# Layer 1's u for the later batches: block products of two levels instead of one, with its steps moved between the products of layer 2

## The chip, the core and the metric

The kernel runs on one core of a Trainium2 chip. The metric is the device time of one execution in microseconds (us). The kernel before took 1878.11 us, the median of three runs (1877.98 to 1878.81). The profiled execution took 1878.7 us; the span between its first and its last instruction is 1876.8 us, and the clock granted to TensorE was 0.999 of full speed.

## The reference

The input x has shape (8, 512, 32, 32): eight batches, 512 channels, 1024 positions, all in float32. Four layers follow each other. Layer 0 mixes the channels through a small attention whose matrix is divided by its largest singular value. Layer 1 is group norm and attention over the 1024 positions, layer 2 a projection to 3 x 128 channels with an attention of its own, layer 3 a convolution with signs as weights. The part that matters here is layer 1:

```
h = _group_norm(x, gamma, beta).reshape(B, C, N)
q = jnp.einsum('oc,bcn->bon', wq, h) + bq[None, :, None]
k = jnp.einsum('oc,bcn->bon', wk, h) + bk[None, :, None]
logits = jnp.einsum('bcn,bcm->bnm', q, k) * scale
attn = jax.nn.softmax(logits, axis=-1)
```

The kernel doesn't form q and k one by one. It multiplies the two weights once into a 512 x 512 matrix wu and computes, for each batch, u = wu h + bias, a 512 x 1024 matrix; the logits are then the product of u and h.

## The kernel before, in words

Up to about 184 us the kernel loads the input, computes layer 0's statistics and the combined weights. Then `fast` (line 911) runs once for each of the eight batches, and for each it runs these stages in turn: layer 1's scores (`scores1`), its value projection (`make_v`), its value products (`values1`, line 566), layer 2's projection (`project2`, line 658), layer 2's scores (`scores2`, line 826), its value products (`values2`, line 981), and layer 3 with the output (`leave`, line 705), half of which is put off into the next batch.

u of batch n+1 is made while layer 2 and layer 3 of batch n run. `make_u` (line 490) is a generator: each `next` issues one step. In `fast` it stands as `steps`, and `fill()` (line 966) asks it for a step at places that the code names: after the last projections of `project2`, after every second row block of `scores2`, before `values2`, between the parts of `leave`, and what is left at the end of the batch. In batch 0 u of the first batch is made ahead of the loop.

Large products are not computed directly. A product of two matrices is cut into 2 x 2 blocks and done with seven block products instead of eight: `sums_of` (line 318) makes the sums of the left factor's blocks (S1 to S4), `differences_of` those of the right factor's (T1 to T4), and `seven` (line 342) issues the seven products and joins them. The seven terms are A11 B11, A12 B21, S1 T1, S2 T2, S3 T3, S4 B22 and A22 T4. Some are summed in place in PSUM: the bank `pa` first takes A11 B11, ScalarE copies it out (`move`), then S2 T2 is added into the same bank and it is copied out again, and so on. `move` runs on ScalarE (lines 350 and 352), `plus`, which adds a bank to what lies in SBUF, on VectorE (lines 356 and 358). For u, `make_u` works on two groups of 128 rows; each of its 14 steps is one term with a contraction of 256, that is two matmuls of 128 x 128 by 128 x 512, and the matmul instructions all have line 405 (`product_of`).

All eight PSUM banks stand in one pool with the tag `bank`. A scheduler orders the instructions of each engine: it follows the program's order as long as operands are ready, and issues what comes later in the program when something before it would have to wait. The order in which it leaves them is then fixed; on the chip each engine works its list off in that order and waits where an operand isn't there. Semaphores guard a PSUM bank as a whole: a product into one half of a bank waits for a reading of the other half.

wu and the sums su of its blocks lie in the pool of the weights for the whole kernel. A fallback at the end (`general`), which runs only if a check on the softmax sums fails, uses wu too.

Of the kernel before, what the change touches and what calls it, by code (L numbers as in the profile page):

```python
# [16 lines left out]
P = 128  # L17
B = 8
C = 512
# [66 lines left out]
def kernel(  # L86
# [157 lines left out]


    r_dram = [dram.tile([4, N // 4], F32, name=f"r_dram{i}") for i in range(2 * B)]
    f_dram = [dram.tile([P, HF], F32, name=f"f_dram{b}") for b in range(B)]
    gm = [keep.tile([P, P], F32, tag=f"gm{j}", name=f"gm{j}") for j in range(NPAIR)]
    gs_, gh_ = (
# [18 lines left out]

    wu = wpool.tile([P, CC, C], F32, tag="wu", name="wu")
# [5 lines left out]
    su = wpool.tile([P, 3, 2, C // 2], F32, tag="su", name="su")  # L277
    so = wpool.tile([P, 3, 2, C // 2], F32, tag="so", name="so")


# [209 lines left out]
    def make_u(env, hb, got, early=False):  # L490
# [32 lines left out]
        for g in groups:  # L523
            yield from g

    def make_v(hb, vt):
# [131 lines left out]
    def project2(env, xt, made):  # L658


        big = env["big"]
        tpg = big.tile([P, 3, N], F32, tag="us", name="tpg")
        tt, pt = tpg[:, 0:1, :], tpg[:, 1:2, :]
        gt = tpg[:, 2, :].rearrange("p (t c) -> p t c", c=P)
        wa = weights["tp"]
        xb = differences_of(
            [xt[:, chunks[k], half(n)] for k in range(2) for n in range(2)],
            [env["e"].tile([P, 2, HF], F32, tag="e", name="xd") for i in range(4)],
        )
        term = product_of(lambda a, b, q, k: wa[a][:, k, :], lambda a, b, q, k: xb[b][:, k, :])  # L670
        yield from seven(
            term,
            tt[:, 0, half(0)],
            tt[:, 0, half(1)],
            pt[:, 0, half(0)],
            pt[:, 0, half(1)],
            col("L2_conv_W_b", 0),
            col("L2_conv_W_b", 1),
        )
        for h in reversed(range(NH)):  # L680
            ps = bank().rearrange("p (t c) -> p t c", c=P)
            for i in range(4):
                for cc in range(CC):
                    mm(  # L684
                        out=ps[:, i, :],
                        lhsT=xt[:, cc, bass.ts(4 * h + i, P)],
                        rhs=sbw["tpg"][:, cc, 2 * P : 3 * P],
                        start=cc == 0,
                        stop=cc == CC - 1,
                    )  # L690
            nc.vector.tensor_tensor(
                gt[:, bass.ts(h, 4), :], ps, bg_row.unsqueeze(1).to_broadcast([P, 4, P]), ALU.add
            )
            yield
        made.extend((tt, pt, gt))
# [130 lines left out]
    def scores2(env, pt, tt, fill):  # L826
        es, esum = [], None
        for t in range(NT):
            e = env["e"].tile([P, N], F32, tag="e", name="e")
            for h in range(NH):  # L830
                ps = bank()
                mm(  # L832
                    out=ps,
                    lhsT=pt[:, 0, bass.ts(t, P)],
                    rhs=tt[:, 0, half(h)],
                    start=True,
                    stop=True,
                )
# [72 lines left out]
    def fast(env, n, hb, ua):  # L911
# [12 lines left out]
        for k, _ in enumerate(scores1(env, hb, ua, es)):  # L924
            if rest3 and k % 2 == 0:
                if next(rest3[0], "end") == "end":
                    rest3.pop()
                    if more and order[n + 1] not in resident:
                        resident[order[n + 1]] = load_x(order[n + 1])
            if n == 0 and k == 2:  # L930
                weights["o"] = sums_of(quarters_of(wo, chunks, cols2), [so[:, i] for i in range(3)], True)
            if n == 0 and k == 6:
# [22 lines left out]
        for k, _ in enumerate(values1(env, xt, vt, es, r, scratch)):  # L955
            chore(k in (2, 7, 9, 11, 13))
            if k == 5 and more:
                nxt = resident[order[n + 1]]
                hb = split_h(env, normal(env, nxt))
        signs = None  # L960
        if more:
            steps = make_u(env, hb, got)
        else:
            signs = unpacked(env)

# [611 lines left out]
    def filler():  # L1577

        yield from natural("v", "k")
        load_w("p", w_p, [P, CC, C], a1, tag="v")
        yield from product(nat["q"], nat["k"], wu, True)
        for b in order[:2]:
# [12 lines left out]
        yield from product(nat["v"], sbw["p"], wo, False)  # L1597
# [35 lines left out]
    with ExitStack() as main:  # L1633
# [8 lines left out]
        for _ in make_u(env, hb, got, True):  # L1642
            pass
        ua = got[0]
        for n in range(B):
            hb, ua = fast(env, n, hb, ua)

# [113 lines left out]
    with tc.If(verdict[0] > 0):  # L1761
        with (
# [5 lines left out]
            env = {"big": big, "e": epool, "small": small}  # L1768
            psum_pools(stack, 2, 4)

            for a in (weights["u"], weights["o"]):
                nc.vector.tensor_tensor(a["S3"], a["A11"], a["S3"], ALU.subtract)
            for b in range(B):
                xt = load_x(b)
                general(env, xt, b, channels(out[b]))
# [42 lines left out]
```

## Time and profile before

| what | value | where it is read |
|---|---|---|
| time, median of three runs | 1878.11 us | the runs |
| time of the profiled execution | 1878.7 us | the profile |
| span of the profiled execution | 1876.8 us | head of the page |
| TensorE busy with matmuls (PE) | 1856.3 us, 99% | part 1 of the page |
| VectorE busy (DVE) | 1118.4 us, 60% | part 1 |
| ScalarE busy (ACT) | 545.4 us, 29% | part 1 |
| GpSimd busy (POOL) | 121.9 us, 6% | part 1 |
| line 405, right factor h, left factor wu (u) | 192 matmuls, 88.9 us busy | groups |
| moved by DMA | 66.51 MB, mean 35 GB/s | part 2 |

A row of the timeline gives the start, the duration, the engine, the line, the operation, the tile that is written and those that are read, the shape and how often it follows itself; in brackets, how long the engine had been idle and what ended that. PE is the matmul, PEld the load of the stationary operand, which runs beside the matmul before. A matmul of the code is two instructions in the trace, so a step of `make_u` is a row with x4. "us, mean ns" of a group are the time in which one or more of its instructions ran, and the mean duration of one; matmuls overlap, so the time from one start to the next is shorter than the duration.

### The profile page before, as it was taken

To read this page: it belongs to the slowest core of one execution; us is meant where nothing else is said; L and a number is where in the kernel's file an instruction comes from. 1 tells how busy PE (TensorE), PEld (TensorE's weight loads), DVE (VectorE), ACT (ScalarE), POOL (GpSimd) and SP (SyncE) were. 2 spreads that over 40 slices of the span, in tenths; PEclk is the share of its full clock that TensorE was granted. 3 is DMA by queue.
4 is the path that set the end of the run, shared out by engine and by line. 5 is a ranking of instruction groups with operands and counts; after the bars stand their busy time and mean duration, and the time that the engine had idled before them with its cause. 6 is when DMAs were issued, how large, how long until landed. Compare 5 with 4: busy or idle time off the path is not lost.

```text
span 1876.8 us, 16564 instructions
## 1 busy us (share of the span) xinstructions
PE 1856.3 (99%) x6244; PEld 952.5 (51%) x6244; DVE 1118.4 (60%) x2077; ACT 545.4 (29%) x888; POOL 121.9 (6%) x109
## 2 busy tenths in 40 slices
PE   9999999999999999999999999999999999999997
PEld 3456465544645455544645455544645464544653
DVE  3347687467754777567764676457643666355447
ACT  2142221244202521244202522144202521244113
POOL 1000001100020001100020001100020001000011
PEclk9999999999999999999999999999999999999999
DMA  8420000002000200002000200001000200000001
GB/s 323 164 79 7 1 18 1 1 34 73 12 1 12 90 18 1 0 34 73 12 1 12 88 19 0 1 34 67 12 0 12 90 12 0 1 34 23 12 0 47
DMA packets 25202, 66.51 MB, mean 35 GB/s; under 512 B 3552, under 2 KB 4764, under 8 KB 24476
## 3 DMA queue, kind: packets, MB, share of 16 engines
q1 hardware_dynamic: 24188, 64.96, 9.6%
q8 instruction: 51, 0.84, 0.2%
q10 hardware_dynamic: 864, 0.43, 0.1%
q14 instruction: 35, 0.29, 0.0%
q0 software_dynamic: 64, 0.00, 0.0%
HBM read 46.44 MB, written 18.94 MB: 35 GB/s over the span
## 4 chain that ended last, share of the span: by engine, by line
PE 96%; DVE 2%; ACT 1%; DMA 0%; issue 0%; POOL 0%; DVEq 0%; ACTq 0%
PE bank L405 46%; PE bank L583 21%; PE bank L832 6%; PE bank L985 5%; PE bank L1372 4%; PE bank L684 3%; PE bank L701 3%; PE bank L429 2%; PE bank L724 1%; PE wide L1417 1%; PE bank L1053 1%; PE bank L1473 1%; PE bank L855 0%; PE quad L1266 0%; PE bank L1563 0%; PE bank L1159 0%
## 5 line engine op out<-in xcount | busy, mean ns | idle before, releaser
L583 PE MATMUL bank<-e,vt 128*128 128x512 f32 x768 | 336.2, 594 | 0.0
L583 PEld LDWEIGHTS bank<-e,vt 128*128 128x128 f32 x768 | 144.3, 190 | 172.3 <-issue 167.9
L405 PE MATMUL bank<-ut,h 128*128 128x512 f32 x384 | 178.9, 597 | 0.0
L405 PEld LDWEIGHTS bank<-ut,h 128*128 128x128 f32 x384 | 71.3, 190 | 94.7 <-issue 93.0
L405 PE MATMUL bank<-us,hs 128*128 128x512 f32 x256 | 115.6, 593 | 0.0
L832 PE MATMUL bank<-tpg 128*128 128x512 f32 x256 | 115.4, 595 | 0.0
L985 PE MATMUL bank<-e,tpg 128*128 128x512 f32 x256 | 114.7, 595 | 0.0
L356 DVE TENSOR_TENSOR e<-bank,e 128x512 f32<-128x512 f32 x96 | 66.1, 689 | 60.8 <-PE bank L405 45.1
L839 ACT ACTIVATE e<-bank 128x512 f32<-128x512 f32 x128 | 76.3, 597 | 67.0 <-PE bank L832 67.0
L350 ACT COPY e<-bank 128x512 f32<-128x512 f32 x96 | 56.2, 585 | 118.8 <-PE bank L405 118.5
L405 PE MATMUL bank<-wo,h 128*128 128x256 f32 x384 | 89.9, 384 | 0.0
L405 PE MATMUL bank<-h,wu 128*128 128x512 f32 x192 | 88.9, 594 | 0.0
L985 PEld LDWEIGHTS bank<-e,tpg 128*128 128x128 f32 x256 | 48.1, 190 | 60.4 <-issue 60.0
L236 POOL TENSOR_TENSOR r_r<-r_v,minus_half 128x4 f32<-128x4 f32 (+1 forms) x11 | 10.9, 989 | 1044.9 <-DVE r_v L235 1039.3
L405 PEld LDWEIGHTS bank<-wo,h 128*128 128x128 f32 x384 | 71.4, 190 | 12.6 <-issue 3.8
L405 PEld LDWEIGHTS bank<-us,hs 128*128 128x128 f32 x256 | 48.4, 190 | 57.5 <-issue 54.5
L844 DVE TENSOR_TENSOR esum<-esum,e 128x1024 f32<-128x1024 f32 x48 | 58.8, 1226 | 30.1 <-ACT e L839 29.9
L712 ACT ACTIVATE sg<-xt,rb 128x512 f16<-128x512 f32 x64 | 44.2, 716 | 107.9 <-DVE xt L703 105.0
L832 PEld LDWEIGHTS bank<-tpg 128*128 128x128 f32 x256 | 47.6, 190 | 55.0 <-issue 52.4
L356 DVE TENSOR_TENSOR vt<-bank,vt 128x512 f32<-128x512 f32 x48 | 33.2, 692 | 66.4 <-PE bank L405 65.5
L350 ACT COPY vt<-bank 128x512 f32<-128x512 f32 x64 | 37.3, 584 | 121.3 <-PE bank L405 121.2
L350 ACT COPY ut<-bank 128x512 f32<-128x512 f32 x48 | 28.1, 586 | 126.9 <-PE bank L405 126.9
(370 smaller groups left out, 2926.4 us busy)
## 6 DMA issues: line engine op xcount, KB each, us to landing
xt<-in_x SPq DMA_DIRECT2D x55, 512.0 KB
out<-both SPq DMA_DIRECT2D x63, 256.0 KB
rfull<-r_dram SPq DMA_DIRECT2D x15, 512.0 KB
f_dram<-f SPq DMA_DIRECT2D x8, 256.0 KB
fb<-f_dram SPq DMA_DIRECT2D x8, 256.0 KB
w<-in_w SPq DMA_DIRECT2D x1, 1024.0 KB
q<-in_w_q SPq DMA_DIRECT2D x1, 1024.0 KB
k<-in_w_k SPq DMA_DIRECT2D x1, 1024.0 KB
```

Source lines behind the costliest of these rows:

```text
L350: nc.scalar.copy(dst, ps)
L356: nc.vector.tensor_tensor(dst, ps, u, ALU.add)
L405: mm(out=ps[:, q * w : (q + 1) * w], lhsT=lt(ka, kb, q, k), rhs=rhs(ka, kb, q, k), start=first and q == 0 and k == 0, stop=last and k == 1 ...
L583: mm(out=ps, lhsT=a[:, t, bass.ts(r_, P)], rhs=e[t], start=first and t == 0, stop=last and t == NTH - 1, skip_group_check=True,)
L684: mm(out=ps[:, i, :], lhsT=xt[:, cc, bass.ts(4 * h + i, P)], rhs=sbw["tpg"][:, cc, 2 * P : 3 * P], start=cc == 0, stop=cc == CC - 1,)
L701: mm(out=ps, lhsT=sbw["z"][:, bass.ts(oc, P)], rhs=att, start=True, stop=True)
L712: nc.scalar.activation(sg[:, cc, :], xt[:, cc, half(h)], AF.Sign, bias=rb3[:, cc : cc + 1])
L832: mm(out=ps, lhsT=pt[:, 0, bass.ts(t, P)], rhs=tt[:, 0, half(h)], start=True, stop=True,)
L839: nc.scalar.activation(e[:, half(h)], ps, AF.Exp, scale=float(P) ** -0.5)
L844: nc.vector.tensor_tensor(esum, esum, e, ALU.add)
L985: mm(out=banks[h], lhsT=gt[:, t, :], rhs=es[t][:, half(h)], start=t == 0, stop=t == NT - 1,)
L1372: mm(out=banks[i][side(h), :], lhsT=w0[i][:, cc, :], rhs=xt[:, cc, half(h)], start=cc == 0, stop=cc == CC - 1,)
```

## The change

`make_u` stays for the first u, ahead of the loop. For the seven later batches `make_u2` takes its place. Each of the seven terms is itself a product of two matrices of 256 x 256 and 256 x 512, and `inner` computes it with seven products again, each one matmul of 128 x 128 by 128 x 256. That is 49 matmuls for each batch where there were 28 of twice the width. An inner product needs two banks: `p1` holds `pa` in its left half and `pc` in its right half, `p2` holds `pb`. Six of the seven products go to `p1`, and after each of them the half that it wrote is read out, by ScalarE or, where the term is added to what stands in u already, by VectorE.

The blocks of wu and their sums for the second level are computed once, on GpSimd, spread over the first batch (`factors_of_u`), and stored to DRAM. For each inner product `prepare_u` loads 7 x 128 x 128 of them again, on the sync engine's queue, and GpSimd makes the differences of the right factor in three instructions of 512, 256 and 256 columns. Two inner products are prepared ahead, and the pool `jit` has two buffers of each kind. Two sums that `seven` took from PSUM, of 128 x 1024 each, are now made on GpSimd from SBUF (`add`).

wu and su lie in a pool of their own, `first_u`, that is closed before the second u is made; `jit` takes its place. wu goes to DRAM for the fallback.

`project2` yields more often (after each of the four position blocks of its g part), `scores2` calls its filler after each half row block, and each of these places asks for one step. There are no fillers left behind the scores: what is left of the steps is issued in one go after `leave`'s first half in the program's order.

```
+    def prepare_u(env, hb, i):
+        jit = env["jit"]
+        fac = jit.tile([P, 7, P], F32, tag="fac", name="fac", bufs=2)
+        nc.sync.dma_start(out=fac, in_=fac_dram[i])
+        b = hb[pairs[i][1]]
+        t = jit.tile([P, 4, QF], F32, tag="jit", name="jit", bufs=2)
+        lo, hi = slice(0, QF), slice(QF, HF)
+        tt = nc.gpsimd.tensor_tensor
+        tt(t[:, 0:2], b[:, :, hi], b[:, 0, :].rearrange("p (i n) -> p i n", i=2), ALU.subtract)
+        tt(t[:, 2], b[:, 1, hi], t[:, 0], ALU.subtract)
+        tt(t[:, 3], b[:, 1, lo], t[:, 2], ALU.subtract)
...
+    def inner(made, d, x=None, bias=None):
+        fac, rhs = made
+        p1, p2 = bank(), bank()
+        lo, hi = slice(0, QF), slice(QF, HF)
+        pa, pc, pb = p1[:, lo], p1[:, hi], p2[:, lo]
...
+        def move(dst, ps, k, i=None):
+            if x is not None:
+                plus(dst, ps, x[k], i)
+            elif bias is None or i is None:
+                nc.scalar.copy(dst, ps)
+            else:
+                nc.scalar.activation(dst, ps, AF.Identity, bias=bias[i])
+        product(pa, 0, True, False)
+        move(d11, pa, 0)
+        product(pc, 3, False, False)
+        move(d22, pc, 3)
+        yield
+        product(pa, 2, False, False)
+        move(d12, pa, 1)
+        product(pc, 4, False, True)
+        plus(d12, pc, d12, 0)
+        yield
+        product(pa, 5, False, False)
+        plus(d22, pa, d22, 1)
+        product(pb, 1, True, True)
+        plus(d11, pb, d11, 0)
+        yield
+        product(pa, 6, False, True)
+        move(d21, pa, 2, 1)
+        yield
+
+    def make_u2(env, hb, got, made):
...
+        how = [
+            (r21, None, None),
+            (r11, r21, top),
+            (r21, r21, None),
+            (r22, None, None),
+            (r12, r21, top),
+            (r21, r21, bottom),
+            (r21, r21, None),
+        ]
+        for i, (d, x, bias) in enumerate(how):
+            for j, _ in enumerate(inner(made[i], d, x, bias)):
+                if j == 3:
+                    if i == 4:
+                        add(c12, c22)
+                    if i == 5:
+                        add(c22, c21)
+                    if i + 2 < 7:
+                        made.append(prepare_u(env, hb, i + 2))
+                    if i == 6:
+                        us = env["big"].tile([P, 3, 2, HF], F32, tag="us", name="us")
+                        got.append(
+                            sums_of(
...
+                yield
...
@@ project2
+                if i < 3:
+                    yield
...
@@ scores2
+                if h == 0:
+                    fill(t, h)
...
-            fill(t)
+            fill(t, 1)
...
@@ fast
-            steps = make_u(env, hb, got)
+            steps = make_u2(env, hb, got, made_u)
...
-        for k, _ in enumerate(project2(env, xt, made)):
-            fill(k > 5)
+        for _ in project2(env, xt, made):
+            fill()
...
-        def between(t):
-            fill(t % 2)
-            chore(t in (1, 3, 5, 7))
+        def between(t, h):
+            fill()
+            chore(h and t in (1, 3, 5, 7))
...
-        fill()
         values2(0, range(0, 2))
...
-            fill()
-            for i, _ in enumerate(leave(env, xt, dst, [0])):
-                fill(2 * (i % 2))
+            for _ in leave(env, xt, dst, [0]):
+                pass
...
-            fill(2)
             for _ in steps:
                 pass
```

More of the change, by code (lines that the diff above doesn't have):

```diff
@@ L246 @@
     r_dram = [dram.tile([4, N // 4], F32, name=f"r_dram{i}") for i in range(2 * B)]
+    wu_dram = dram.tile([P, CC, C], F32, name="wu_dram")
+    fac_dram = [dram.tile([P, 7, P], F32, name=f"fac_dram{i}") for i in range(7)]
     f_dram = [dram.tile([P, HF], F32, name=f"f_dram{b}") for b in range(B)]
@@ L267 @@
     bb2 = const.tile([P, CC], F32, tag="bb2", name="bb2")
-    wu = wpool.tile([P, CC, C], F32, tag="wu", name="wu")
+    first_u = ExitStack()
+    upool = first_u.enter_context(
+        tc.tile_pool(name="first_u", bufs=1, side="right", reuse_waits="tile")
+    )
+    wu = upool.tile([P, CC, C], F32, tag="wu", name="wu")
     wo = wpool.tile([P, CC, C], F32, tag="wo", name="wo")
@@ L275 @@
     bvo = const.tile([P, CC], F32, tag="bvo", name="bvo")
-    su = wpool.tile([P, 3, 2, C // 2], F32, tag="su", name="su")
+    su = upool.tile([P, 3, 2, C // 2], F32, tag="su", name="su")
     so = wpool.tile([P, 3, 2, C // 2], F32, tag="so", name="so")
@@ L524, in make_u, with factors_of_u @@
             yield from g
+    pairs = [
+        ("A11", "B11"),
+        ("A12", "B21"),
+        ("S2", "T2"),
+        ("S1", "T1"),
+        ("S4", "B22"),
+        ("S3", "T3"),
+        ("A22", "T4"),
+    ]
+    blocks = {"A11": 0, "A12": 1, "A22": 2, "S1": 3, "S2": 4, "S3": 5, "S4": 6}
+    QF = HF // 2
+    def factors_of_u(env):
+        tt = nc.gpsimd.tensor_tensor
+        for i, (a, _) in enumerate(pairs):
+            w = weights["u"][a]
+            a11, a12, a21, a22 = (w[:, k, bass.ts(m, P)] for m in range(2) for k in range(2))
+            s = env["small"].tile([P, 4, P], F32, tag="half_a", name="factors")
+            tt(s[:, 0], a21, a22, ALU.add)
+            tt(s[:, 1], s[:, 0], a11, ALU.subtract)
+            tt(s[:, 2], a11, a21, ALU.subtract)
+            tt(s[:, 3], a12, s[:, 1], ALU.subtract)
+            nc.sync.dma_start(out=fac_dram[i][:, 0:2], in_=w[:, :, 0:P])
+            nc.sync.dma_start(out=fac_dram[i][:, 2], in_=a22)
+            nc.sync.dma_start(out=fac_dram[i][:, 3:7], in_=s)
+            yield
@@ new lines, in prepare_u @@
+    def prepare_u(env, hb, i):
[5 more added lines that the diff above has]
+        lo, hi = slice(0, QF), slice(QF, HF)
+        tt = nc.gpsimd.tensor_tensor
+        tt(t[:, 0:2], b[:, :, hi], b[:, 0, :].rearrange("p (i n) -> p i n", i=2), ALU.subtract)
+        tt(t[:, 2], b[:, 1, hi], t[:, 0], ALU.subtract)
+        tt(t[:, 3], b[:, 1, lo], t[:, 2], ALU.subtract)
+        rhs = {
+            "B11": b[:, 0, lo],
+            "B21": b[:, 1, lo],
+            "B22": b[:, 1, hi],
+            "T1": t[:, 0],
+            "T3": t[:, 1],
+            "T2": t[:, 2],
+            "T4": t[:, 3],
+        }
+        return fac, rhs
@@ new lines, in inner, with product, plus @@
+    def inner(made, d, x=None, bias=None):
[3 more added lines that the diff above has]
+        pa, pc, pb = p1[:, lo], p1[:, hi], p2[:, lo]
+        (d11, d12), (d21, d22) = ((d[i][:, lo], d[i][:, hi]) for i in range(2))
+        if x is not None:
+            x = [t[:, c] for t in x for c in (lo, hi)]
+        def product(out, k, first, last):
+            a, b = pairs[k]
+            mm(
+                out=out,
+                lhsT=fac[:, blocks[a], :],
+                rhs=rhs[b],
+                start=first,
+                stop=last,
+                skip_group_check=True,
+            )
+        def plus(dst, ps, t, i=None):
+            if bias is None or i is None:
+                nc.vector.tensor_tensor(dst, ps, t, ALU.add)
+            else:
+                nc.vector.scalar_tensor_tensor(dst, ps, bias[i], t, ALU.add, ALU.add)
+        def move(dst, ps, k, i=None):
+            if x is not None:
+                plus(dst, ps, x[k], i)
+            elif bias is None or i is None:
+                nc.scalar.copy(dst, ps)
+            else:
+                nc.scalar.activation(dst, ps, AF.Identity, bias=bias[i])
[17 more added lines that the diff above has]
+        yield
@@ new lines, in make_u2, with quarter, rows, add @@
+    def make_u2(env, hb, got, made):
+        ut = env["big"].tile([P, CC, N], F32, tag="uv", name="ut")
+        top, bottom = ([bu[:, 2 * k + i : 2 * k + i + 1] for i in range(2)] for k in range(2))
+        def quarter(k, h):
+            return ut[:, chunks[k], half(h)]
+        def rows(k, h):
+            return [ut[:, 2 * k + i, half(h)] for i in range(2)]
+        def add(dst, x):
+            nc.gpsimd.tensor_tensor(dst, dst, x, ALU.add)
+        c12, c21, c22 = quarter(0, 1), quarter(1, 0), quarter(1, 1)
+        r11, r12, r21, r22 = (rows(k, h) for k in range(2) for h in range(2))
+        how = [
[6 more added lines that the diff above has]
+            (r21, r21, None),
+        ]
+        for i, (d, x, bias) in enumerate(how):
[11 more added lines that the diff above has]
+                            sums_of(
+                                quarters_of(ut, chunks, [half(0), half(1)]),
+                                [us[:, k] for k in range(3)],
+                            )
+                        )
+                yield
@@ L690, in project2 @@
                     )
+                if i < 3:
+                    yield
             nc.vector.tensor_tensor(
@@ L931, in fast @@
                 weights["o"] = sums_of(quarters_of(wo, chunks, cols2), [so[:, i] for i in range(3)], True)
+            if n == 0 and k in (9, 11, 13, 15, 17, 19, 21):
+                next(late_u)
             if n == 0 and k == 6:
@@ L959, in fast @@
                 hb = split_h(env, normal(env, nxt))
+                if "jit" not in env:
+                    first_u.close()
+                    env["jit"] = main.enter_context(
+                        tc.tile_pool(name="jit", bufs=1, side="right", reuse_waits="tile")
+                    )
+                made_u = [prepare_u(env, hb, i) for i in range(2)]
         signs = None
         if more:
-            steps = make_u(env, hb, got)
+            steps = make_u2(env, hb, got, made_u)
         else:
@@ L1583, in filler @@
         yield from product(nat["q"], nat["k"], wu, True)
+        nc.sync.dma_start(out=wu_dram, in_=wu)
         for b in order[:2]:
@@ L1644 @@
         ua = got[0]
+        late_u = factors_of_u(env)
         for n in range(B):
@@ L1769 @@
             psum_pools(stack, 2, 4)
-            for a in (weights["u"], weights["o"]):
-                nc.vector.tensor_tensor(a["S3"], a["A11"], a["S3"], ALU.subtract)
+            wu = big.tile([P, CC, C], F32, tag="wu", name="wu_again")
+            nc.sync.dma_start(out=wu, in_=wu_dram)
+            a = weights["o"]
+            nc.vector.tensor_tensor(a["S3"], a["A11"], a["S3"], ALU.subtract)
             for b in range(B):
```

## Prediction

> **What bounds the kernel.** First the head of the page, the busy times and the chain that ended last:
>
> ```profile
> span 1876.8 us, 16564 instructions
> ...
> PE 1856.3 (99%) x6244; PEld 952.5 (51%) x6244; DVE 1118.4 (60%) x2077; ACT 545.4 (29%) x888; POOL 121.9 (6%) x109
> ...
> PE 96%; DVE 2%; ACT 1%; DMA 0%; issue 0%; POOL 0%; DVEq 0%; ACTq 0%
> ```
>
> TensorE is the bound, with 96% of the chain. A busy PE can still hide short waits, since one matmul's duration reaches into the next one. So next the timeline of PE in batch 1, where u's steps (h or hs with wu or su) stand between layer 2's products:
>
> ```profile
> 560.17 1.88 PE L405 MATMUL bank<-xd,tpg 128*128 128x512 f32 x4
> 561.88 1.88 PE L405 MATMUL bank<-h,wu 128*128 128x512 f32 x4
> 563.60 3.73 PE L684 MATMUL bank<-tpg,xt 128*128 128x128 f32 x32
> 567.17 1.88 PE L405 MATMUL bank<-hs,su 128*128 128x512 f32 x4
> 568.89 3.73 PE L684 MATMUL bank<-tpg,xt 128*128 128x128 f32 x32
> 572.46 1.88 PE L405 MATMUL bank<-hs,su 128*128 128x512 f32 x4
> ```
>
> The starts give the pace: four instructions of 512 columns take 1.715 us (561.88 to 563.60), 0.429 each; 32 of 128 columns take 3.57, 0.112 each. No start is late: PE has no wait here that could be won. The change can gain by fewer columns alone, and lose by every wait it brings.
>
> The pace at 256 columns, and the way from a product to its reader, stand in the value projection of the same batch (all engines):
>
> ```profile
> 487.48 1.89 PE L405 MATMUL bank<-wo,h 128*128 128x256 f32 x8
> ...
> 489.21 0.33 PE L1053 MATMUL bank<-cur,gm 128*128 128x64 f32 x2
> ...
> 489.41 0.59 ACT L350 COPY vt<-bank 128x512 f32<-128x512 f32 x1 [1.14 <-PE bank L405]
> ```
>
> Eight take 1.73 us, 0.216 each, half of 0.429. The eighth starts at 487.48 + 7 x 0.216 = 488.99, its reader at 489.41, 0.42 later. How a product goes on after its reader, batch 0 shows:
>
> ```profile
> 258.02 0.68 DVE L356 TENSOR_TENSOR e<-bank,e 128x512 f32<-128x512 f32 x1
> ...
> 258.76 0.30 PEld L405 LDWEIGHTS bank<-ut,hs 128*128 128x128 f32 x2 [0.69 <-DVE e L356]
> 258.76 1.55 PE L405 MATMUL bank<-ut,hs 128*128 128x512 f32 x3
> ...
> 259.30 0.19 PEld L405 LDWEIGHTS bank<-ut,hs 128*128 128x128 f32 x1 [0.24 <-issue]
> ```
>
> The reader ends at 258.71, the weight load starts 0.05 later. The next instruction starts at 259.30, so the waiting one streamed from 259.30 - 0.43 = 258.87, 0.11 after its load began.
>
> **The change, part by part.** *Fewer columns.* For each of seven batches 14 steps x 4 instructions x 0.429 = 24.0 us go, and 49 products x 2 x 0.216 = 21.2 us come: -2.86, in all **-20.0 us**, all of it on PE's path.
>
> *Waits on the bank.* Of 49 products 35 follow another one of the same inner product in bank p1 and wait until it is read. From the end of the first one's issue that takes 0.42 - 0.216 + reader + 0.05 + 0.11 = 0.37 + reader. The readers have 256 columns, for which no row stands; by those of 64 and 512 columns (copies on ScalarE 0.21 and 0.585; VectorE 0.23 and 0.69, with a bias 0.74) they take 0.37 on ScalarE, 0.42 or 0.47 on VectorE. So PE needs other work of 0.74, 0.79 or 0.84 us between the two. The order in which PE's instructions stand in the changed kernel tells how much there is: one 512-column matmul (0.858) in 9 to 12 places of a batch and more than that in most others, which is enough; but while the g part of the projection runs, three matmuls of 128 columns (3 x 0.224 = 0.672) in seven places and 0.656 in one. There PE stands: twice 0.07 (ScalarE), three times 0.12, once 0.13, twice 0.17: 0.97 in a batch, **+6.8 us** in all. Below it is 0, if the readers are quicker; above, if the whole 0.22 between a load and its matmul in other rows counts instead of 0.11, the 0.858 places fall short too, and it is 16.
>
> *VectorE's queue.* u's readers on VectorE become 41 of 256 columns, 18 us a batch, for 6 of 0.74; ScalarE's 8 x 0.37 for 8 x 0.59. Between 761 and 820 us VectorE is busy for 28.2 of 59 us; it will be some 47 (18 - 4.5, and u's four sums, 4 x 1.22, move into this stage). It isn't the bound, but its queue is in order, and the sums of layer 2's scores (esum, 1.226 us, seven in a batch) stand between u's readers.
>
> *GpSimd.* Seven times 1.26 + 0.63 + 0.63 and two sums of 2.5 (1.26 us for 512 columns, by the quick rows of line 622) make 22.6 us a batch, which PE's 60 us of this stage could hide. But two views of one moment, VectorE's and GpSimd's timelines in batch 1, show:
>
> ```profile
> 516.56 1.21 DVE L625 TENSOR_TENSOR vt<-vt,scratch 128x1024 f32<-128x1024 f32 x1
> 517.69 2.35 DVE L627 TENSOR_TENSOR e<-e,scratch 128x512 f32<-128x512 f32 x2
> ```
>
> ```profile
> 516.78 2.12 POOL L622 TENSOR_TENSOR xt<-xt,o_b 128x512 f32<-128x512 f32 x1 [3.16 <-issue]
> ```
>
> GpSimd's add takes 2.12 where it takes 1.26 alone, and VectorE's two 2.35 where two take 1.29 (513.61): they run one after the other. VectorE instructions that read PSUM are not slowed (line 654: 0.69 beside GpSimd and without it). So esum and GpSimd's new work take turns, and u's readers queue behind. I lay out the order of batches 4 to 6 from the end of the fifth inner product's last term (A22 T4) at 0. GpSimd: the preparation for the seventh (1.26, 0.63), the first sum (2.5), the preparation's rest (0.63), the second sum (2.5), which needs the sixth inner product. VectorE asks for an esum at 1.1, gets it at 1.5, when GpSimd's first piece ends, and the two readers behind it end at 3.7; S3 T3 of the sixth, due at 3.0, starts at 3.9: 0.9 late. The second sum starts once A22 T4 of the sixth is added, at 7.6 behind another esum, and with a further esum in its way it and the seventh's first reader, which may not overwrite its operand before, end at 12.0; S1 T1 of the seventh, due at 9.9, starts at 12.1: 2.2 late. In batches 0 to 3 what counts is the cover between the sixth's last term and that S1 T1: 3.9 us in batches 0 and 1, 2.4 to 2.6 in 2 and 3; needed are 0.21 + 0.42 + 2.5 + 0.42 + 0.16 = 3.7, and up to 1.2 more behind an esum, so about 0.5 and 2.0 late, and I add 0.6 for lateness of the S3 T3 kind. Together 3 x 3.1 + 2 x 1.1 + 2 x 2.6 = 16.7, 2.4 a batch: **+17 us**. Below, 0.5 a batch (3.5), if esum and GpSimd don't meet; above, 3.5 (24.5), if each turn goes against VectorE.
>
> The Trainium skill states it as a rule in "SBUF — State Buffer", section "Who interferes with whom": a VectorE instruction with two SBUF inputs and a GpSimd instruction that reads SBUF exclude each other for the whole instruction, and whichever starts first blocks the other. The rows agree, and the rule speaks against this change: by it each of three esums could wait out a whole 2.5 us sum, an estimate of 7 us a batch and a kernel at about 1910; by the layout above they meet the shorter pieces more often.
>
> *DMA.* 49 loads of 448 KB each. The nearest, rfull of 512 KB, is issued at 603.79 and its user starts at 607.72: under 4 us. Cover between a buffer's last use and the next first product is 4 to 10 us, 3.4 at the least, where GpSimd is late anyway: 0, or 0.5 a batch without that. On SP's queue the next batch's second factor load now stands between the store of the reciprocals and rfull, and waits for u's last product. PE had 0.5 us to spare before the z products that need rfull (attention ready at 608.41, PE there at 608.90); six u products add 0.9 of cover, the load takes up to 2: I take 0.2 a batch, **+1.4 us** (0 to 5).
>
> *Layer 3.* The steps leave `leave`; its second z products now stand 8 x 0.216 = 1.7 us behind the value products instead of 6.9. They need 0.4 + 0.7 + 0.2 = 1.3: nothing, or 0.6 a batch if VectorE is one instruction behind (0 to 4). The first batch's factors lie on GpSimd and SP beside scores: nothing.
>
> The sum: -20.0 + 6.8 + 17 + 1.4 = +5.2, a span of 1882.0. Time and span of the profiled execution differ by 1.9, and its time is 0.6 above the median: **1883 us**.
>
> **The rivals.** *The cover holds (faster).* PE loses almost nothing in this stage before the change. If GpSimd's pieces and esum rarely meet, only the short covers and 0.5 a batch are left: -20 + 6.8 + 3.5 = -9.7, 1868 us. It decides where the GpSimd waits fall under 0.9 us a batch. Against it: VectorE's and GpSimd's work in those 20 us is nearly continuous.
>
> *Gain and waits cancel.* With 1.7 a batch for GpSimd: -20 + 6.8 + 12 + 1 = 0, 1878.
>
> *The products aren't cheaper.* If 256-column products between others run at the 0.222 mean of some rows of the value projection, the gain shrinks by 98 x 7 x 0.006 = 4 us, and with the upper waits on the bank (16): -16 + 16 + 17 + 1 = +18, 1896 us. The steady 0.216 speaks against it.
>
> **How the numbers follow.** About 0.2% (3.8 us) is what a measurement of this kernel can tell from no change. The forecast, slower by about 5 us, has a chance of 0.46, the faster rival 0.29, the cancelling one 0.19, the dear products 0.06. Faster 0.29, same 0.19, slower 0.52. The bounds added up reach from 1862 to 1908; they won't all fall on one side, so the range is 1864 to 1903.
>
> **What would show it.** PE's u rows: starts 0.43 apart for a pair, and gaps of 0.1 to 0.2 us in the g part. esum's rows: some of 1.8 us and more instead of 1.226. PE idle 1 to 3 us before S1 T1 of the seventh inner product, with GpSimd's sum as what ended it. If esum stays at 1.226 and PE's chain stays without gaps, the GpSimd step is wrong and the time is near 1868.

## The result and the profile after

The changed kernel takes 1966.51 us (median of four runs, 1965.46 to 1968.12), the kernel before beside it 1878.46 us: a ratio of 1.0469, 95% interval 1.0451 to 1.0487. The profiled execution took 1965.78 us with a span of 1963.9 us; the clock granted to TensorE was 0.984. Slower was right, 1883 us and the range up to 1903 were not: 88 us came where 5 were forecast.

The head of the page after, and its chain that ended last:

```profile
span 1963.9 us, 17838 instructions
...
PE 1878.4 (96%) x6538; PEld 1013.1 (52%) x6538; DVE 1241.2 (63%) x2322; ACT 529.6 (27%) x888; POOL 343.4 (17%) x298
...
PE 87%; DVE 8%; ACT 3%; issue 1%; DMA 1%; POOL 0%; SPq 0%; ACTq 0%; DVEq 0%; POOLq 0%
```

TensorE has fallen from 96% to 87% of the chain; VectorE and ScalarE came in. VectorE's share of busy time barely moved (60 to 63%), so the question is where on the path it stands. The groups with an idle time ahead of them tell that (last column: idle time of the engine before them, and who ended it; the first block is the kernel before, whose line 724 became line 881, the second the changed kernel):

```profile
L724 PE MATMUL bank<-sg,sw 128*128 128x512 f16 x112 | 28.7, 379 | 0.0
```

```profile
L595 PE MATMUL bank<-jit,fac 128*128 128x256 f32 x392 | 122.9, 396 | 14.5 <-DVE ut L606 9.1
...
L881 PE MATMUL bank<-sg,sw 128*128 128x512 f16 x112 | 37.1, 433 | 46.9 <-ACT sg L869 46.5
...
L1003 DVE TENSOR_TENSOR esum<-esum,e 128x1024 f32<-128x1024 f32 x48 | 72.0, 1499 | 5.3 <-ACT e L996 5.2
```

u's products (L595) wait, and esum has gone from 1.226 to 1.499 us, both as forecast. But most of the idle time that is new stands at L881, layer 3's sign products, where the kernel before had none: TensorE waits there for the signs of the second half. TensorE's timeline at the end of batch 0:

```profile
418.36 1.89 PE L881 MATMUL bank<-sg,sw 128*128 128x512 f16 x8
420.44 3.70 PE L858 MATMUL bank<-att,z 128*128 128x512 f32 x8 [0.19 <-DVE att L1162]
423.98 1.88 PE L411 MATMUL bank<-ut,h 128*128 128x512 f32 x4
432.50 1.81 PE L881 MATMUL bank<-sg,sw 128*128 128x512 f16 x3 [6.65 <-ACT sg L869]
434.11 1.91 PE L411 MATMUL bank<-us,hs 128*128 128x512 f32 x2
```

6.65 us idle, in each of seven batches. What VectorE did in that time:

```profile
418.56 1.23 DVE L329 TENSOR_TENSOR us<-ut 128x1024 f32<-128x1024 f32 x1 [2.74 <-PE bank L1153]
419.70 0.68 DVE L1162 TENSOR_TENSOR att<-bank,rfull 128x512 f32<-128x512 f32 x1
420.30 1.22 DVE L332 TENSOR_TENSOR us<-us,ut 128x1024 f32<-128x1024 f32 x1
421.44 1.22 DVE L333 TENSOR_TENSOR ut<-ut 128x1024 f32<-128x1024 f32 x1
422.57 1.22 DVE L334 TENSOR_TENSOR us<-ut,us 128x1024 f32<-128x1024 f32 x1
423.70 0.76 DVE L893 TENSOR_SCALAR both<-both 128x512 f32<-128x512 f32 x2
...
428.22 0.68 DVE L860 TENSOR_TENSOR xt<-bank,xt 128x512 f32<-128x512 f32 x1
...
432.67 0.68 DVE L860 TENSOR_TENSOR xt<-bank,xt 128x512 f32<-128x512 f32 x1
```

and ScalarE, which makes the signs out of L860's results:

```profile
426.40 1.39 ACT L924 ACTIVATE up<-both,cb 128x512 f32<-128x512 f32 x2 [5.37 <-DVE both L902]
...
431.75 1.93 ACT L869 ACTIVATE sg<-xt,rb 128x512 f16<-128x512 f32 x3
...
434.05 0.72 ACT L869 ACTIVATE sg<-xt,rb 128x512 f16<-128x512 f32 x1
```

VectorE works without a break from 418.56 to 433.35 us. First come u's four sums (L329 to L334, 4.9 us): u is now complete before the end of layer 2's value products, and its sums, whose tile stands where those products' operand stood until 418.5 us, are the first thing VectorE may do behind them (the value products, line 1153, are what ends the 2.74 us of idle time before L329). Then layer 3's first half, and among it the four additions of layer 2's second half (L860). ScalarE is idle for 5.37 us, waiting for VectorE, and then has L924 and L925 in front of the signs. In the kernel before the sums stood behind the four additions (there line 703):

```profile
413.42 0.68 DVE L703 TENSOR_TENSOR xt<-bank,xt 128x512 f32<-128x512 f32 x1
...
415.34 1.88 DVE L703 TENSOR_TENSOR xt<-bank,xt 128x512 f32<-128x512 f32 x3
...
418.45 1.21 DVE L323 TENSOR_TENSOR us<-ut 128x1024 f32<-128x1024 f32 x1
```

### The profile page after: what moved, and what is told of

It reads as the page before. It is cut to its first block, busy times and chain, and to the rows that moved or that the text cites. A ratio compares the mean times of both kernels' runs of the same rounds, so it can differ in the third digit from the quotient of the medians.

```text
span 1963.9 us, 17838 instructions
## 1 busy us (share of the span) xinstructions
PE 1878.4 (96%) x6538; PEld 1013.1 (52%) x6538; DVE 1241.2 (63%) x2322; ACT 529.6 (27%) x888; POOL 343.4 (17%) x298
## 4 chain that ended last, share of the span: by engine, by line
PE 87%; DVE 8%; ACT 3%; issue 1%; DMA 1%; POOL 0%; SPq 0%; ACTq 0%; DVEq 0%; POOLq 0%
PE bank L411 36%; PE bank L738 20%; PE bank L595 7%; PE bank L1153 5%; PE bank L1537 4%; PE bank L989 3%; PE bank L839 3%; DVE esum L1003 2%; PE bank L858 2%; PE bank L435 2%; PE bank L881 1%; PE wide L1582 1%; ACT up L924 1%; ACT both L925 1%; PE bank L1014 1%
## 5 line engine op out<-in xcount | busy, mean ns | idle before, releaser
L606 DVE TENSOR_TENSOR ut<-bank,ut 128x256 f32<-128x256 f32 x203 | 84.0, 420 | 100.0 <-PE bank L595 94.2
L595 PE MATMUL bank<-jit,fac 128*128 128x256 f32 x392 | 122.9, 396 | 14.5 <-DVE ut L606 9.1
L989 PE MATMUL bank<-tpg 128*128 128x512 f32 x256 | 127.1, 595 | 0.0
L411 PE MATMUL bank<-us,hs 128*128 128x512 f32 x256 | 126.9, 635 | 0.0
L595 PEld LDWEIGHTS bank<-jit,fac 128*128 128x128 f32 x392 | 64.9, 188 | 93.0 <-issue 41.4
L356 ACT COPY e<-bank 128x512 f32<-128x512 f32 x96 | 56.0, 583 | 115.3 <-PE bank L411 114.9
L411 PEld LDWEIGHTS bank<-us,hs 128*128 128x128 f32 x256 | 52.8, 207 | 65.2 <-issue 58.4
L881 PE MATMUL bank<-sg,sw 128*128 128x512 f16 x112 | 37.1, 433 | 46.9 <-ACT sg L869 46.5
L1003 DVE TENSOR_TENSOR esum<-esum,e 128x1024 f32<-128x1024 f32 x48 | 72.0, 1499 | 5.3 <-ACT e L996 5.2
L839 PEld LDWEIGHTS bank<-tpg,xt 128*128 128x128 f32 x512 | 71.6, 191 | 5.2 <-issue 0.5
```

What stands on the lines that cost most here:

```text
L411: mm(out=ps[:, q * w : (q + 1) * w], lhsT=lt(ka, kb, q, k), rhs=rhs(ka, kb, q, k), start=first and q == 0 and k == 0, stop=last and k == 1 ...
L595: mm(out=out, lhsT=fac[:, blocks[a], :], rhs=rhs[b], start=first, stop=last, skip_group_check=True,)
L606: nc.vector.tensor_tensor(dst, ps, t, ALU.add)
L839: mm(out=ps[:, i, :], lhsT=xt[:, cc, bass.ts(4 * h + i, P)], rhs=sbw["tpg"][:, cc, 2 * P : 3 * P], start=cc == 0, stop=cc == CC - 1,)
L881: mm(out=ps, lhsT=lt[:, cc, bass.ts(j, P)], rhs=sg[:, cc, :], start=cc == 0, stop=cc == CC - 1,)
L989: mm(out=ps, lhsT=pt[:, 0, bass.ts(t, P)], rhs=tt[:, 0, half(h)], start=True, stop=True,)
```

## The experiments

Two theories at the start. **Cover**: the seven steps of u that left layer 3's stage (12 us of TensorE's work) had hidden its latency (the first expectations call this the placement theory). **Queue**: VectorE and ScalarE take their work in the wrong order now. A third, **two levels**, puts the loss on u's new products. Medians in us; the kernel before took 1878.5 to 1879.4 beside them. The kernel without GpSimd's part in u isn't in the table; its time is told below.

| kernel | time | ratio to before, 95% |
|---|---|---|
| one level, the change's placement | 1949.4 | 1.0357 to 1.0391 |
| the same, sums later | 1902.3 | 1.0110 to 1.0141 |
| the same, layer 2 closed first, with the first signs earlier | 1892.6 | 1.0059 to 1.0086 |
| the same, pairs kept together | 1887.1 | 1.0028 to 1.0057 |
| two levels, the change | 1966.5 | 1.0451 to 1.0487 |
| signs later | 1966.3 | 1.0444 to 1.0479 |
| old places | 1977.6 | 1.0500 to 1.0537 |
| sums later | 1920.1 | 1.0198 to 1.0232 |
| layer 2 closed first | 1925.4 | 1.0201 to 1.0262 |
| third bank | 1958.1 | 1.0402 to 1.0439 |
| sums on VectorE | 1954.8 | 1.0390 to 1.0422 |
| four edits | 1888.1 | 1.0031 to 1.0061 |
| and the first signs earlier | 1887.2 | 1.0029 to 1.0056 |
| and pairs kept together | 1882.2 | 1.0003 to 1.0022 |
| and pauses behind the sums | 1883.6 | 1.0018 to 1.0036 |

**One level, the change's placement.** The kernel before, with the change's edits in `project2` and `scores2`, a step of `make_u` at every second filler, and this:

```
-            fill()
-            for i, _ in enumerate(leave(env, xt, dst, [0])):
-                fill(2 * (i % 2))
+            for _ in leave(env, xt, dst, [0]):
+                pass
...
-            fill(2)
```

> The kernel before with the change's placement alone: u stays with one level of blocks, and its 14 steps go between the products of layer 2's projection and scores; none is left behind the scores. Placement theory (the loss is that layer 3's stage lost the matmuls that covered the wait for the second half's signs): TensorE waits about 6.6 us in a batch for the second half's signs, as in the changed kernel (56 us there in seven batches), some 9 us follow from the lower granted clock behind it, 4 us in front of the second z products; 1878 + 55 to 75 = 1933 to 1953 us. Two-level theory (the loss is in u's products with their waits and loads): no such products here, 1875 to 1885 us.

1949.4 us, and the same wait to the hundredth of a microsecond:

```profile
430.34 1.81 PE L726 MATMUL bank<-sg,sw 128*128 128x512 f16 x3 [6.65 <-ACT sg L714]
```

So 70 of the 88 us (1949.4 against 1879.4 beside it) come without any two-level product: the two-level theory is out for these. Cover and queue are not told apart yet.

**Signs later.** `k % 2 == 0 and k >= 6` where the sign products are called, with TensorE in the program's order for the first twelve steps of the scores.

> The changed kernel, but the second half's sign products stand 14 matmuls later in TensorE's order, behind 16 instead of 2 matmuls of the next batch's scores, and TensorE keeps the program's order over those first 12 steps of the scores. 12 x 0.429 = 5.1 to 14 x 0.429 = 6.0 us more cover. Placement theory: of 6.65 us of wait in a batch 0.6 to 1.5 are left, and the lower clock behind it goes for the most part; 1966 - 40 to - 55 = 1911 to 1926 us. Two-level theory: 1966 us, within 5.

1966.3 us, no gain at all. (The expectation priced a matmul of the code as one instruction; it is two, so the added cover was even twice as long.) The wait only changed its place:

```profile
426.94 1.88 PE L411 MATMUL bank<-us,hs 128*128 128x512 f32 x4
435.44 3.60 PE L411 MATMUL bank<-us,hs 128*128 128x512 f32 x4 [6.62 <-ACT e L356]
```

TensorE could run ahead for eight instructions; then the next product waits for a copy (L356) that stands in ScalarE's order behind layer 3's work. Other TensorE work needs the same two engines, and they are late. That is against cover.

**Sums later.** `make_u2` hands out `ut`, and `sums_of` is called behind `next(rest3[0])`; the scheduler puts two of the four sums behind L860, and `att` ahead of all.

> The changed kernel, but the four sums of u's blocks (1.22 us each on VectorE) are issued by the program behind layer 3's second half; two of them then stand behind the second half's xt adds in VectorE's order, two still in front of layer 3's first instructions. If VectorE's queue makes the signs late (the sums stand in front of layer 3's work, 418.6 to 423.8 us in batch 0), the signs come 2.45 us earlier in each of seven batches: 1966 - 17 = 1949 us, 1943 to 1953 with the clock. If ScalarE's or TensorE's order alone makes them late, under 4 us of gain: 1962 to 1967 us.

1920.1 us: 46 us, more than twice the 17 expected. I had counted only the two sums that went behind; a third had moved behind layer 3's first instruction too, which starts at 419.66 instead of 423.70 us, and ScalarE takes the first sign at 426.22 instead of 431.75. TensorE's wait before it is 2.22 us. The gain is what the queue theory asks for. With one level:

> The kernel before with the change's placement (one level of blocks, 1949 us), and u's four sums behind layer 3's second half in the program. Queue theory (the sums in front of layer 3 in VectorE's order are most of what the placement costs): as in the kernel with two levels, where this edit took 46 us: 1949 - 46 = 1903 us, 1896 to 1910, the rest being what the missing cover costs by itself. Cover theory: 1940 to 1949 us.

1902.3 us, 47 less, as the queue theory had it.

**Old places.** Two levels at the fillers of the kernel before, two steps for each old one.

> The changed kernel's products of two levels, with its steps at the places of the kernel before, two for each old one: 16 in the projection and the scores, 12 behind them. Cover theory (the 12 us of TensorE's work that left layer 3's stage are the loss): the wait for the signs (56 us), the lower clock behind it (9) and the wait of the z products (4) go, 1966 - 69 = 1897 us, 1888 to 1910. Queue theory (what binds that stage is the work in VectorE's and ScalarE's order): three inner products bring some 20 readings of 0.42 us, 8 us a batch, into the same queues, and most of the cover is used up by that: 1920 to 1950 us.

1977.6 us: the cover is back, and the kernel is slower than with none. The wait for the signs is gone (idle time before the sign products 0.0), but TensorE now waits 62 us in all before u's products, nearly all of it for their readers on VectorE, where it waited 16 in the changed kernel. The expectation's queue theory was right in direction and too small, since u's own readings stand behind layer 3's. VectorE, GpSimd and TensorE of this kernel:

```profile
428.56 2.31 DVE L891 TENSOR_SCALAR both<-both 128x512 f32<-128x512 f32 x1 [0.45 <-ACT both L890]
430.91 0.69 DVE L892 SCALAR_TENSOR_TENSOR both<-both,bank 128x512 f32<-128x512 f32 x1
431.52 0.41 DVE L606 TENSOR_TENSOR ut<-bank,ut 128x256 f32<-128x256 f32 x1
```

```profile
428.26 2.34 POOL L649 TENSOR_TENSOR ut<-ut 128x1024 f32<-128x1024 f32 x1 [5.38 <-DVE ut L608]
```

```profile
431.99 1.22 PE L595 MATMUL bank<-jit,fac 128*128 128x256 f32 x2 [4.18 <-DVE ut L606]
```

GpSimd's sum starts 0.3 us before L891, an instruction of 0.42 us elsewhere, and L891 ends 0.27 us behind the sum (2.3 us in 7 of 28 cases, once a batch); u's reader L606 stands behind it, and TensorE waits 4.18 us. L891 has a single input in SBUF. The Trainium skill, "SBUF — State Buffer", section "Who interferes with whom", says that such an instruction is blocked by GpSimd only if it runs in a mode that takes both of VectorE's ports, which tensor_scalar can enter; the 2.31 us fit that, though no row names the mode.

**Layer 2 closed first.** The second half's z products and signs stand in front of layer 3's first half in the program:

```
-            for _ in leave(env, xt, dst, [0]):
-                pass
+            first = leave(env, xt, dst, [0], stop=True)
+            next(first)
             close2(xt, att, 1)
             rest3.append(leave(env, xt, dst, [1], stop=True))
             next(rest3[0])
+            for _ in first:
+                pass
```

> The changed kernel with layer 2's second half closed, and the second half's signs taken, in front of layer 3's first half in the program; nothing is left out. The second half's z products and xt adds then stand in front of layer 3's first half in TensorE's and VectorE's order. Queue theory (the signs wait since VectorE has u's four sums and layer 3's first half, 4.9 and 8 us, in front of the xt adds): the signs are there when TensorE asks; the z products pay 1.3 to 2.4 us a batch, as they follow the value products at once: 1966 - 56 - 9 + 9 to 17 = 1910 to 1920 us. Cover theory (whatever comes first, TensorE lacks work of its own while the two others finish layer 3): the wait only moves on, 1955 to 1970 us.

1925.4 us. The wait for signs is gone (idle time before L881 0.0) with not one matmul of cover given back; the z products pay 2.0 us a batch: as in the changed kernel `att` stands behind one of the sums, but no sign products stand between the value products and the z products any more, which covered that:

```profile
420.41 5.37 PE L858 MATMUL bank<-att,z 128*128 128x512 f32 x8 [2.01 <-DVE att L1162]
```

**Third bank.** `pc` in a bank of its own, opened with `start`.

> The changed kernel with pc in a third bank, so that an inner product's pa and pc don't wait for each other's reading. Waits of u's products that are under 0.15 us each come to some 15 us more than the kernel before has of such. Bank theory (they are waits on the shared bank, 6.8 to 16 us by the prediction): 1966 - 7 to - 15 = 1951 to 1959 us. If a pause of that length is only the pace of 256-column products, or if three banks at a time instead of two make the pool short: 1964 to 1972 us.

1958.1 us: 8.4 us less, the price of the shared bank.

**No GpSimd in u.**

> The changed kernel without GpSimd's part in u: the differences of the right factor's blocks and the two sums on GpSimd are left out, the block products take plain blocks of h in their place (so u, and with it the output, is another). Taking-turns theory of the prediction (GpSimd's sums and esum exclude each other, 17 us, 2.4 a batch): esum falls from a mean of 1.50 back to 1.23 us and the waits of u's products on VectorE fall from some 33 to some 8 to 16 us; 1966 - 17 to - 25 = 1941 to 1949 us. Bank theory (the waits of u's products are for readers of the same bank and for VectorE's longer queue): under 8 us of gain, 1958 to 1966 us.

Its u is another, so the softmax sums fail their test and the execution goes on into the fallback; 4232.8 us is the time of both. So the two kernels are compared at the last batch's first z product. In the changed kernel and in this one:

```profile
1934.18 3.17 PE L858 MATMUL bank<-att,z 128*128 128x512 f32 x7
```

```profile
1910.28 3.17 PE L849 MATMUL bank<-att,z 128*128 128x512 f32 x7
```

23.9 us, and esum is quick again:

```profile
L994 DVE TENSOR_TENSOR esum<-esum,e 128x1024 f32<-128x1024 f32 x48 | 58.4, 1218 | 3.1 <-ACT e L987 2.9
```

**Sums on VectorE**, GpSimd's differences left where they are:

> The changed kernel with the two sums of 128 x 1024 in u on VectorE instead of GpSimd, nothing else. Taking-turns theory as the prediction laid it out (most of the 17 us come from the two sums of 2.5 us in the way of esum and u's readers): 1966 - 8 to - 14 = 1952 to 1958 us. If GpSimd's many short differences do it, or the sums cost VectorE as much as they cost in turns: 1963 to 1968 us.

1954.8 us: 11.7 us, half of GpSimd's price, come from the two sums.

**Four edits together, and the first signs earlier** (a second `next(first)` in front of `close2`, so that sign products cover the wait for `att`), with two levels and with one:

> The changed kernel with four edits together: u's four sums behind layer 3's second half in the program, layer 2 closed first, pc in a third bank, and the two sums of 128 x 1024 on VectorE (1.22 us) instead of GpSimd (2.5). Queue theory and the sizes measured so far: 1966 - 46 (sums later, measured) - 10 (rest of the waits for signs, less the z products' new wait) - 10 (bank) - 8 (half of GpSimd's 17) = 1892 us, 1880 to 1905. Cover theory: not under 1915 us.

> The four edits together (1888 us), and the first sign products in front of the second half's z products, so that these don't wait 0.95 us a batch for the attention rows. 6.9 us of waiting go: 1888 - 7 = 1881 us, 1876 to 1886. Beside the one-level kernel with the same edits it gives the price of the two levels alone: by the terms measured so far (-20 of columns, +8 of bank waits left, +8 of GpSimd's, +3 of rest) about 0.

> The same, with layer 2's second half closed in front of layer 3's first half too, and only the first sign products in front of that. Queue theory: no wait for signs or z products is left although the cover is gone, and one level with the change's placement comes back to the kernel before: 1878 us, 1875 to 1886. Cover theory: not under 1900 us.

1888.1, 1887.2 and 1892.6 us. Earlier signs took the wait of the z products away (idle time 5.5 us before the edit, 0.0 after it), but the time went down by only 0.9; the intervals of these two overlap. The one-level kernel has no wait over 0.5 us in this stage and was expected at 1878; 14 us were open. A part stood in a row that I had not looked at, layer 0's products for the next batch:

```profile
1299.02 1.12 PE L429 MATMUL bank<-fb,pv 64*128 64x512 f32 x2
1300.07 1.99 PE L405 MATMUL bank<-ut,hs 128*128 128x512 f32 x4
1301.98 1.98 PE L429 MATMUL bank<-fb,pv 64*128 64x512 f32 x6
```

These have 64 rows. Torn apart, two and six of them take 1.05 + 1.91 us from start to start; in one piece eight take 1.91 (next kernel), 0.24 each. A matmul of 128 rows and 512 columns takes 0.43, so those that follow each other overlap two at a time:

```profile
1300.75 1.99 PE L429 MATMUL bank<-fb,pv 64*128 64x512 f32 x8
1302.66 1.55 PE L405 MATMUL bank<-us,hs 128*128 128x512 f32 x3
```

Closing layer 2 first, with the first signs earlier, had torn them: over the whole kernel these products are busy for 32.6 us in the kernel before, in the changed kernel and in both kernels with the sums later, and for 40.1 us in the one-level kernel with layer 2 closed first.

**Pairs kept together**: `k in (10, 15, 21, 27)` for layer 0's steps.

> One level of blocks with the change's placement and all order edits (1892.6 us), and layer 0's second and third step for the next batch at the fifteenth and twenty-first step of the scores instead of the thirteenth and twentieth, so that its products of 64 rows, which run two at a time, aren't torn apart by others in TensorE's order (1.05 us a batch, seven batches). Torn-pairs theory: 1892.6 - 7 = 1885 us, 1883 to 1888. If the rest of the 14 us is that layer 3's second half is still late: 1890 to 1894 us.

> The same edit in the kernel with two levels and all edits (1887.2 us). Torn-pairs theory: 1887 - 7 = 1880 us, 1878 to 1883. Else 1885 to 1889 us.

1887.1 and 1882.2 us, 5.5 and 5.0 less. One of the eleven executions of the two-level kernel took 4378 us. The only other kernel here of such a length is the one that goes on into the fallback (4232.8 us); whether this execution did so, and why, is open, and it would have to be cleared up before anyone used that kernel. The last one, with the spare fillers as pauses:

> That, and the three places of the fillers that u's 28 steps leave over used as pauses behind u's two sums (one behind the first, two behind the second), so that the next inner product doesn't stand behind them at once. u's products wait 8.5 us in the kernel with all edits, 0.9 a batch of it behind the second sum, 2.7 once in the first batch. If cover is what is short there: 1880 - 4 to - 7 = 1873 to 1876 us, under the kernel before. If VectorE's queue as a whole is full there: 1879 to 1882 us.

1883.6 us: no gain. TensorE's idle time before u's products, where their readers end it, fell from 6.0 to 3.6 us, and that in the chains of layer 0's singular values, which wait for VectorE, rose from 5.2 to 8.2. That speaks for VectorE's queue as a whole and against missing cover, without proving it. No version beats the kernel before.

## Why the prediction was wrong, step by step

| step | forecast, us | measured, us | by |
|---|---|---|---|
| fewer columns | -20.0 | -18.9 | u's rows in batch 4 of the two kernels with all edits, from start to start: 24.0 to 21.3 us (22.2 less a wait of 0.9), times 7 |
| waits on the bank | +6.8 (0 to 16) | +8.4 | third bank |
| GpSimd and esum | +17 (3.5 to 24.5) | +23.9 | no GpSimd in u |
| DMA | +1.4 (0 to 5) | +1.0 | z products behind rfull: 0.76 in batch 4, 0.23 in batch 5 |
| layer 3 | 0 (0 to 4) | +70 | one level, the change's placement |

Together 84 of 88; the rest is not put down to a row, and edits need not add up exactly. Without the last row it would be +14: that the change makes the kernel slower was forecast for reasons that held.

The step that failed is "Layer 3", with the sentence on VectorE's queue. It asked only whether the second z products come too early behind the value products, and found 1.7 us of cover for 1.3 of need (the z products did lose some 0.35 us a batch by the starts, behind a sum). It did not follow the z products on to what hangs on them: the additions on VectorE, the signs on ScalarE, the second half's sign products. That chain needs both engines at once, and the four sums stood at its head. The prediction had counted them into the stage of the projection and the scores (its "this stage", 761 to 820 us); but their tile is free only when the last value product has read its operand, so they start where layer 3 does (418.56 us in batch 0). "It isn't the bound" was true of VectorE's share and false of its order. By the one-level runs the 70 us are 47 for the sums in front, 15 for layer 2's second half behind layer 3's first (closing it first won 10, and 5.5 more once the pairs that this edit had torn were together), and 8 that stay open. My own first reading after the result, missing cover, fell as well: more matmuls stood in front of the waiting product in two kernels, and neither got faster. That u's steps in the kernel before hid nothing isn't shown by that; there their few long readings and the sums at the end left VectorE in time.

The other steps were right in kind. The rows named as signs came: esum 1.499 us, u's products idle for 1.0 to 2.0 us once in a batch (twice in the first) and for 0.25 to 0.5 us at least once. What ends the long wait is a reader on VectorE (L606, once L608), not GpSimd's sum itself; in batch 4 it stands behind an esum of 3.18 us that runs beside the sum. GpSimd cost 24 instead of 17, at the upper bound: 3.4 us a batch, so the faster rival, which needed under 0.9, was far off. The products were not dear: 21.3 us for 98 instructions are 0.217 each. At equal placement the two levels cost 17 us where the forecast had 5 (1949.4 to 1966.5); with a third bank, the sums on VectorE and the order mended they win 5 (1892.6 to 1887.2, and 1887.1 to 1882.2), which the rest of the placement eats up.

## What to carry to other kernels

When work moves out of a stage, follow every chain that crosses it to its end, engine by engine in the order of the queues, and look at what the move puts at the head of a queue, not at the engine's share of busy time. A wait of TensorE is cured by more TensorE work only if that work does not need the late engines itself; here moving sums out of the head of a queue was worth 47 us over seven batches, and 10 us more of matmuls in front of the waiting product in each batch nothing. An order that fits one place can undo another: look afterwards at rows that the edit did not touch.

## What the runs showed of the hardware

A wait costs more than its length. The changed kernel's windows behind the wait (columns: window, its length, busy time and instructions of PE, PEld, DVE, ACT, POOL, then the granted clock):

```profile
432.00:437.00 5.00, 4.44 (x8) 1.79 (x8) 1.35 (x3) 3.29 (x6) 0.00 (x0) 0.55 0.27 105
437.00:442.00 5.00, 5.00 (x15) 2.17 (x14) 2.86 (x5) 3.63 (x7) 0.00 (x0) 1.00 0.00 0
```

In the first of these windows, right behind the pause, the clock is 0.55, and the two matmuls of 512 columns from 434.11 to 435.81 us start 0.85 us apart instead of 0.43; with seven pauses that is some 9 us of the 88, by the starts of the products behind them. Pauses of 2.2 us can have it behind them too: with the sums later the clock is 0.60 from 429 to 432 us, and in six of the seven batches the eight matmuls behind the pause take 4.9 to 5.1 us from start to start instead of 3.43. In the one-level kernel with the same pause it is three of seven batches; what decides it isn't shown. The Trainium skill, "TensorE: Matmul & The Clock Gate", section "What's actually happening", has the clock halved after an idle window of about 3.4 us; here it was halved behind pauses of 2.2 us as well.
